# A gated-attention kernel: the row-tiled products of a group in one run, with another set of order keys

## The chip, the cores and the metric

The kernel runs on one core of a Trainium2 chip. The metric is the device time of one execution in microseconds (us). Five engines take part, each working through its own list of instructions in order: TensorE (PE, matrix products), VectorE (DVE), ScalarE (ACT), GpSimd (POOL) and SyncE (SP), which here issues nearly all DMA transfers. Engines wait for each other only through semaphores.

## The reference, cut to what matters

```python
xn = layernorm(x)                                  # x: 4 batch rows x 512 positions x 256
Q = xn @ Wq + bq                                   # 16 heads of 128
K, V = xn @ Wk + bk, xn @ Wv + bv                  # 4 key heads; each serves 4 query heads
attn = softmax(Q @ K.T / sqrt(128) + causal_mask)  # per head, 512 x 512
ctx = attn @ V
y = gelu(ctx @ Wo + bo)
s = layernorm(xn + y) * gamma + beta
g = silu((silu(gate) * up) @ w_down.T)             # gate, up = halves of xn @ w_gate_up.T
out = x + s * g
```

Everything is float32. The kernel writes each float32 operand of most products as a sum of a leading part and a rest in a shorter format, and forms three products per pair (leading x leading, leading x rest, rest x leading).

## The kernel before, in words

Up to about 101 us the kernel loads and splits weights, normalizes x and runs the feed-forward part of the earlier batch rows. Attention then runs in 16 groups, one for each batch row (4) and key head (4): `ph = b * 4 + g`, in `order.run()`. A group has these steps; the short names are those of the tasks.

- `Qp`, `Kp`, and once a batch row `Vp`: projections on TensorE, copied out of PSUM in two parts by ACT (`Qh`, `Kh`, `Vh`) and DVE (`Ql`, `Kl`, `Vl`). The four `Qp` of a group use the four PSUM banks `bank0` to `bank3`.
- `Sp` (line 703): scores. A product covers 32 queries of each of the four heads against the keys that they may see; 4 row blocks `i` of 128 queries with 4 such products `t` each, into PSUM tiles `ps`, of which there are two. `M` on DVE adds the mask and takes the row's least value, `E` on ACT takes the exponential into the tile `p` and sums the row, `R` on DVE inverts the sum, and `N` (line 746) on POOL normalizes.
- `T` (line 760) on DVE transposes a 128 x 512 piece of `p` in 32 x 32 blocks into one of four tiles `u`. `H` (line 789) on ACT copies its leading part to `pT`, and `L` (line 792) on POOL writes the rest. There are ten such pieces in a group, (i, j) with key tile j not above row block i: four for j = 0, three for j = 1, two for j = 2, one for j = 3.
- `W` (`weighted`, line 798): the weights times the values, as products with 32 rows in four row tiles of the array at once, one for each head, adding up in `bank0` to `bank3`. The values of a group, `vr`, are loaded in two halves by SP (`values_beside`, line 663; four transfers for each half).
- `Ch` on ACT and `Cl` on DVE copy the banks to `ctxT`; `Y` on TensorE multiplies with `w_o`, adding up over the four groups of a batch row in `py`.
- After a batch row's last group, `O`, `G` and the `F` tasks (partly on POOL) form GELU, the second normalization and the output.

The order of all instructions is fixed when the program is written. The class `Order` holds a list of tasks, each with its engine, an estimated duration, a key, the tasks that it comes after, and places in rings that it takes and gives back. `Order.run` (line 81) plays them through: whenever an engine is free, it emits the ready task with the smallest key. `keep` chains each engine's instructions in the order found. The estimates set only this order; on the chip an instruction waits for the data and buffers that it really uses. The keys are sums of the numbers in `KEYS` and of the group number; for instance, where `ph` is the group:

```python
key = ph - 0.3 + K["t0"] + K["t1"] * j + K["t2"] * i       # T
... key + K["h"] ...  key + K["l"]                          # H, L
ph + (K["w0"] if ph + 2 < NPH else K["lw"]) + K["w1"] * m   # W
base = ph - 0.5 + K["s0"] + ... K["s1"] * i                 # Sp, M, E
```

How many runs `W` is cut into is set by `RUNS` (line 24): each entry is a list of key tiles whose products are emitted without anything between. Four places use it:

```python
runs = ((3,), (2,), (1,), (0,)) if last else RUNS            # line 1119
deps = [(x, b, g, i, j) for j in run for i in range(j, NT) for x in "HL"] + [("vr", b, g, j // 2) for j in run]
done_w[ph] = {j: ("W", b, g, m) for m, run in enumerate(runs) for j in run}   # line 1135
slot = [done_w[ph - 1][j]] if ph else ...                    # line 1114: what H of tile j waits for
```

So a run comes after the `H` and `L` of its own tiles, and the next group's `H` for tile j comes, in the planned order, after the run that holds j. `Ch` comes after a group's last run. The loads of `vr` come after the runs of the group before that hold the same tiles. The last group (15) always has four runs, one tile each. The tiles `pT` and `vr` and the loaded weights `w_q` and `w_o` share 13 buffers of one kind.

Of the kernel before, what the change touches and what calls it, by code (L numbers as in the profile page):

```python
# [19 lines left out]
EPS = 1e-5  # L20
S = 32
MASK = -1e9
KEYS = {"q0": 1.294, "q1": -0.162, "k": 1.154, "v0": 2.242, "v1": -0.947, "s0": -2.531, "s1": 0.181, "s2": -0.026, "n": -5.223, "t0": -5.822, "t1": 3.68, "t2": 2.849, "h": 1.078, "l": -1.275, "w0": -1.75, "w1": -0.111, "c": 3.151, "y0": 0.375, "y1": 1.022, "f0": 1.31, "f1": 4.659, "wo": 28.733, "wq": 2.307, "vr": 3.547, "ls": 2.337, "lt": -16.381, "lc": 7.543, "lw": 2.356, "da": 2.973, "db": 1.284}
RUNS = ((0, 1), (2, 3))
ON_ACT = (0, 1)
HIGHEST = 3.4028235e38

# [132 lines left out]
def kernel(  # L160
# [803 lines left out]
    for name, n in (("s", 2), ("u", 4), ("ctx", 3), ("gate", 2), ("stage", 1)):  # L964
        order.ring(name, n)
    K = KEYS
    weights, done_w = {}, {}
# [52 lines left out]
    for ph in range(NPH):  # L1020
# [97 lines left out]
        last = ph + 1 == NPH  # L1118
        runs = ((3,), (2,), (1,), (0,)) if last else RUNS
        for m, run in enumerate(runs):  # L1120
# [125 lines left out]
```

## Time and profile before

| what | value |
|---|---|
| median of 3 runs | 639.38 us (638.06 to 639.59) |
| the profiled execution, its own time | 637.73 us |
| its span, first to last instruction | 635.8 us |
| mean granted TensorE clock | 0.994 |
| TensorE matmul, busy | 616.7 us (97%) |
| POOL, DVE, ACT, busy | 455.7, 417.6, 405.0 us |
| row-tiled products (`bank<-pT,vr`) | 3072, 120.7 us busy |
| score products (`ps<-kT,qT`) | 576, 115.0 us busy |
| output products (`py<-w_o,ctxT`) | 768, 112.7 us busy |

A line of the profile names an engine, an operation and its tiles as out<-in. Nearly all lines stand under L49, because the helper at line 49 records every instruction; the tile names tell them apart. Matmuls are pipelined and overlap, so the length of a step on TensorE is read from one step's start to the next step's start, not from busy time. PEclk is the granted TensorE clock, 1.00 being full speed. "x192" counts instructions. In a table by stretch each engine's busy us are followed by its number of instructions.

### The profile page before, as it was taken

What the parts mean: (1) busy time and instruction counts of PE and PEld (TensorE: products, weight loads), DVE (VectorE), ACT (ScalarE), POOL (GpSimd) and SP (SyncE); (2) the same over time, 40 slices, a digit from 0 to 9 for tenths busy, and PEclk for the clock granted to TensorE, in tenths of its full rate; (3) what the DMA queues carried; (4) which work ended last, traced back from release to release, by engine and by line L of the source; (5) the groups of instructions that cost most, each with busy time, mean ns of one, the idle gap of its engine ahead of it and who ended that gap; (6) DMA issues with size and microseconds to landing.
All of it is one profiled execution on the core that took longest, in us unless ns stands there. A gap on an engine that the chain in (4) does not pass through costs nothing.

```text
span 635.8 us, 15865 instructions
## 1 busy us (share of the span) xinstructions
PE 616.7 (97%) x6004; PEld 552.4 (87%) x6004; DVE 417.6 (66%) x1131; ACT 405.0 (64%) x1025; POOL 455.7 (72%) x595
## 2 busy tenths in 40 slices
PE   7999998999999999999999999999999999999994
PEld 6888886988988889899888989888999988998894
DVE  5974517465439585668669584877767587768635
ACT  3542415484259686778858595977668598758652
POOL 4698778173516985949599794959996586999653
PEclk9999998999999999999999999999999999999998
DMA  6867788407398369553967867196947818774900
GB/s 206 275 197 242 269 283 283 159 4 204 103 318 220 111 163 257 165 138 95 294 186 174 241 175 234 34 299 182 231 170 184 245 55 253 174 197 109 262 5 34
DMA packets 86236, 118.09 MB, mean 186 GB/s; under 512 B 5648, under 2 KB 72336, under 8 KB 82064
## 3 DMA queue, kind: packets, MB, share of 16 engines
q1 hardware_dynamic: 86160, 117.08, 64.0%
q8 instruction: 47, 0.77, 0.5%
q14 instruction: 29, 0.24, 0.1%
HBM read 87.70 MB, written 29.36 MB: 184 GB/s over the span
## 4 chain that ended last, share of the span: by engine, by line
PE 65%; POOL 12%; DMA 9%; DVE 6%; issue 4%; ACT 2%; SPq 2%; POOLq 0%; DVEq 0%; ACTq 0%
PE bank L49 30%; PE ps L49 13%; PE py L49 10%; POOL pT L49 4%; PE pd L49 4%; PE pv L49 3%; PE pk L49 3%; DMA vr<-v_dram 3%; POOL p L49 2%; DMA fin_dram<-gate 1%; DMA xT_dram<-xT 1%; DVE p L49 1%; DMA fin<-fin_dram 1%; POOL gate L539 1%; POOL w_d L246 1%
## 5 line engine op out<-in xcount | busy, mean ns | idle before, releaser
L49 POOL TENSOR_SCALAR p<-p,total 128x384 f32<-128x384 f32 (+7 forms) x248 | 118.7, 499 | 68.9 <-DVE total L49 68.6
L49 ACT ACTIVATE p<-p,least 128x192 f32<-128x192 f32 (+15 forms) x256 | 131.7, 516 | 56.8 <-DVE least L49 52.0
L49 DVE CUSTOM_DVE_ANT_0 p<-ps,mask 128x192 f32<-128x192 f32 (+15 forms) x256 | 104.4, 431 | 77.7 <-PE ps L49 76.5
L49 PE MATMUL bank<-pT,vr 32*128 32x128 f32 (+15 forms) x3072 | 120.7, 307 | 0.2 <-DMA vr<-v_dram 0.2
L49 PEld LDWEIGHTS bank<-pT,vr 32*128 32x128 f32 x3072 | 113.0, 184 | 7.6 <-issue 2.9
L49 PE MATMUL ps<-kT,qT 128*128 128x512 f32 (+11 forms) x576 | 115.0, 332 | 3.0 <-DVE least L49 2.4
L49 POOL TENSOR_TENSOR pT<-u,pT 128x512 fp32r<-128x512 f32 x83 | 107.2, 1299 | 12.1 <-ACT pT L49 10.7
L49 PE MATMUL py<-w_o,ctxT 128*128 128x256 f32 x768 | 112.7, 286 | 1.1 <-DVE ctxT L49 1.0
L49 POOL TENSOR_TENSOR pT<-u_more,pT 128x512 fp32r<-128x512 f32 x77 | 99.6, 1299 | 13.3 <-PE bank L49 8.3
L49 PEld LDWEIGHTS py<-w_o,ctxT 128*128 128x128 f32 x768 | 103.2, 189 | 4.3 <-DVE ctxT L49 1.5
L49 PEld LDWEIGHTS ps<-kT,qT 128*128 128x128 f32 x576 | 87.0, 188 | 14.1 <-DVE least L49 8.0
L49 PE MATMUL bank<-xT_again,w_q 128*128 128x512 f32 x384 | 95.0, 393 | 0.0
L49 PEld LDWEIGHTS bank<-xT_again,w_q 128*128 128x128 f32 x384 | 71.3, 189 | 14.2
L49 ACT CAST pT<-u 128x512 fp32r<-128x512 f32 x83 | 51.3, 619 | 26.4 <-DVE u L49 20.4
L49 DVE STREAM_TRANSPOSE u<-p 128x512 f32<-128x512 f32 x83 | 57.7, 698 | 10.2 <-POOL p L49 9.0
L49 DVE STREAM_TRANSPOSE u_more<-p 128x512 f32<-128x512 f32 x77 | 54.0, 701 | 13.7 <-POOL p L49 8.0
L49 ACT ACTIVATE ctxT<-bank,bv_sb 128x512 fp32r<-128x512 f32 x64 | 42.3, 683 | 27.1 <-PE bank L49 25.2
L49 ACT CAST pT<-u_more 128x512 fp32r<-128x512 f32 x77 | 47.1, 619 | 13.6 <-DVE u_more L49 8.5
L49 DVE SCALAR_TENSOR_TENSOR ctxT<-bank,bv_sb,ctxT 128x512 fp32r<-128x512 f32 x64 | 46.3, 738 | 9.5 <-ACT ctxT L49 9.5
L49 POOL TENSOR_TENSOR y<-y,fin 128x256 f32<-128x256 f32 x40 | 29.5, 739 | 29.7 <-ACT y L49 11.8
L49 DVE SCALAR_TENSOR_TENSOR qT<-bank,bq_sb,qT 128x384 fp32r<-128x384 f32 x64 | 38.5, 602 | 18.3 <-ACT q L49 18.2
L49 ACT ACTIVATION_READ_ACCUMULATOR p<-p,least 128x1 f32 x256 | 48.2, 188 | 0.0
(134 smaller groups left out, 951.0 us busy)
## 6 DMA issues: line engine op xcount, KB each, us to landing
vr<-v_dram SPq DMA_DIRECT2D x128, 256.0 KB, 7.0
w_q<-w_dram_q SPq DMA_DIRECT2D x15, 1024.0 KB, 5.3
w_o<-w_dram_o SPq DMA_DIRECT2D x15, 1024.0 KB, 10.0
v_dram<-v SPq DMA_DIRECT2D x16, 512.0 KB, 3.6
fin<-fin_dram SPq DMA_DIRECT2D x16, 384.0 KB, 5.5
xT_dram<-xT SPq DMA_DIRECT2D x8, 512.0 KB, 4.9
fin_dram<-gate SPq DMA_DIRECT2D x16, 256.0 KB, 4.3
xT_again<-xT_dram SPq DMA_DIRECT2D x8, 512.0 KB, 4.2
```

The source lines that it names most:

```text
L49: made = getattr(self.engine, name)(*args, **kw)
L246: lo_on.tensor_tensor(dst[1], src, dst[0].bitcast(F32), ALU.subtract)
L539: pool.tensor_tensor(g[:, 1 + k], g[:, 0], gb_sb[:, k], ALU.mult)
```

## The change

`RUNS` has one entry in place of two: the row-tiled products of all four key tiles form one run, which comes after all ten `H` and `L` and after both halves of `vr`. `done_w` then names this one run for every tile. All thirty numbers in `KEYS` are other ones; among them `w0` goes from -1.75 to -6.162, `h` from 1.078 to 7.725, `s0` from -2.531 to -1.292 and `q0` from 1.294 to 0.186. The last group's four runs stay. No instruction is added or taken out.

```diff
--- before.py
+++ after.py
@@ -20,8 +20,8 @@
 EPS = 1e-5
 S = 32
 MASK = -1e9
-KEYS = {"q0": 1.294, "q1": -0.162, "k": 1.154, "v0": 2.242, "v1": -0.947, "s0": -2.531, "s1": 0.181, "s2": -0.026, "n": -5.223, "t0": -5.822, "t1": 3.68, "t2": 2.849, "h": 1.078, "l": -1.275, "w0": -1.75, "w1": -0.111, "c": 3.151, "y0": 0.375, "y1": 1.022, "f0": 1.31, "f1": 4.659, "wo": 28.733, "wq": 2.307, "vr": 3.547, "ls": 2.337, "lt": -16.381, "lc": 7.543, "lw": 2.356, "da": 2.973, "db": 1.284}
-RUNS = ((0, 1), (2, 3))
+KEYS = {"q0": 0.186, "q1": 0.188, "k": 1.276, "v0": 2.664, "v1": -0.427, "s0": -1.292, "s1": 0.081, "s2": 0.03, "n": -5.947, "t0": -4.154, "t1": 2.359, "t2": 2.218, "h": 7.725, "l": -1.068, "w0": -6.162, "w1": 1.004, "c": 3.429, "y0": 0.388, "y1": 1.235, "f0": 1.568, "f1": 3.265, "wo": 26.284, "wq": 4.081, "vr": 4.774, "ls": 2.625, "lt": -17.512, "lc": 4.554, "lw": 2.179, "da": 4.28, "db": 1.598}
+RUNS = ((0, 1, 2, 3),)
 ON_ACT = (0, 1)
 HIGHEST = 3.4028235e38
```

## The prediction

> **What bounds the kernel now.** I read the page's busy shares first, then a table of busy times by stretch, then TensorE's timeline around the row-tiled products.
>
> ```profile
> span 635.8 us, 15865 instructions
> PE 616.7 (97%) x6004; PEld 552.4 (87%) x6004; DVE 417.6 (66%) x1131; ACT 405.0 (64%) x1025; POOL 455.7 (72%) x595
> ```
>
> A busy share alone proves little, so here are four groups of the second batch row, one group to a line (from the start of one group's first run of row-tiled products to the next). The columns are the stretch, its length, and the busy us of each engine.
>
> ```profile
> core 0: us, PE busy (x) PEld busy (x) DVE busy (x) ACT busy (x) POOL busy (x), PEclk, DMA share, GB/s
> 327.45:356.40 28.95, 28.77 (x352) 26.27 (x355) 20.56 (x67) 20.58 (x62) 27.60 (x38) 1.00 0.72 197
> 356.40:385.30 28.90, 28.90 (x329) 26.09 (x325) 19.65 (x51) 20.52 (x52) 23.12 (x29) 1.00 0.75 218
> 385.30:414.30 29.00, 29.00 (x305) 26.90 (x298) 20.66 (x69) 22.21 (x65) 19.56 (x27) 1.00 0.39 107
> 414.30:443.25 28.95, 28.66 (x317) 25.19 (x316) 21.95 (x60) 22.90 (x51) 21.83 (x31) 1.00 0.88 245
> ```
>
> TensorE idles 0.5 us of 115.8 here. So between about 105 and 595 us the time is the length of TensorE's instruction stream; only what shortens or stalls that stream counts. POOL stands second and in the first of these lines (groups 5, 9 and 13, where the previous batch row's final normalization is also done) it is at 27.60 of 28.95.
>
> Now the price of one change between 128-row and 32-row products. TensorE's timeline (start, length, what, how many):
>
> ```profile
> 354.21 4.64 PE L49 MATMUL bank<-pT,vr 32*128 32x512 f32 x96
> 358.79 0.95 PE L49 MATMUL ps<-kT,qT 128*128 128x256 f32 x6
> 359.67 2.88 PE L49 MATMUL bank<-pT,vr 32*128 32x256 f32 x96
> 362.47 0.79 PE L49 MATMUL ps<-kT,qT 128*128 128x192 f32 x5
> ```
> ```profile
> 304.18 7.27 PE L49 MATMUL bank<-pT,vr 32*128 32x512 f32 x192
> 311.38 0.83 PE L49 MATMUL ps<-kT,qT 128*128 128x416 f32 x3
> ...
> 412.58 0.84 PE L49 MATMUL ps<-kT,qT 128*128 128x256 f32 x6
> 413.26 0.53 PE L49 MATMUL py<-w_o,ctxT 128*128 128x256 f32 x3
> ```
>
> From start to next start, the split group takes 4.58 (tiles 0 and 1) + 0.88 (two score products between) + 2.80 (tiles 2 and 3) = 8.26 us. In one stretch the 192 products take 311.38 - 304.18 = 7.20, and the same two score products, among 128-row neighbours, 413.26 - 412.58 = 0.68: together 7.88. One round trip into row tiles and back costs 8.26 - 7.88 = **0.38 us**.
>
> **The change, part by part.**
>
> *Two runs become one.* The timeline shows which groups are really split. Groups 1, 4, 8 and 12 already run as one stretch (starts 215.75, 304.18, 420.20, 536.04), because their second run happened to be placed straight after the first. Group 15 keeps its four runs in both kernels. Eleven groups are split (0, 2, 3, 5, 6, 7, 9, 10, 11, 13, 14). Removed: 11 x 0.38 = **4.2 us** of TensorE's stream. No product, load or copy is removed or added; 3072 row-tiled products stay.
>
> *The new wait.* The run now needs all ten probability tiles, so TensorE's row-tiled products of key tiles 0 and 1 wait for the last tile's split on POOL (1.30 us each). Behind that wait on TensorE's queue stand the next group's scores, and this group's context copies on ACT and DVE, its output products and the queries two groups on. What must fill TensorE until then? In group 6 the first run started at 354.21 and the second at 359.67, so at most 4.6 us of other work must be drawn forward. The next group's score rows 1 and 2 are at hand: they stand right behind the first run today (331.96 to 336.7 in group 5, 4.7 us), and DVE and ACT have 6 to 9 us of slack per group. I take 0. If that cover is gone, the cost is up to 4.6 us a group.
>
> *Splits come later.* In the planned order, a next group's splits for tiles 0 and 1 may start only after the whole run, not after its first part. Between two runs there would be 28.95 - 0.38 - 7.20 = 21.4 us. Ten splits take 13.0 us, normalizing row 3 takes 2.5 (four at 0.63), and the first copy on ACT 0.6: 16.1 us, hidden with 5 us to spare. In groups 5, 9 and 13 the cover is thin (second rival).
>
> *The keys.* `w0` from -1.75 to -6.16 puts the run ahead of the next group's scores (key ph-2.03 before, ph-0.79 after, against ph-1.75 and ph-6.16 for the run): the scores no longer slip in between. `h` from 1.08 to 7.73 puts the first copies of turned tiles behind the next group's exponentials on ACT. Late next: the split on POOL, then the run. Bounded by one or two exponentials (0.6 us each) per tile below, by ACT's idle 6 to 8 us a group above; ACT's slack absorbs it, so I take 0, the nearer end, with up to +1 us a group where POOL is full. `q0`, `k`, `v0`, `y1` reorder fillers among themselves; the same products are issued, so 0, with single stalls of the 0.2 us kind seen at 335.60 either way.
>
> *The sync queue.* Both halves of the values beside the weights (`vr`, eight transfers) now follow the end of the whole run. Their issue took 5.4 us at 423.56 and 10.6 at 185.37, landing 7.0: 12 to 18 us, against the 21 us until the next run. Hidden; if not, a stall like those before the runs of groups 8 and 12 follows, where today the first stretch takes 7.87 and 7.73 instead of 7.20 (0.67 and 0.53 us). `vr` at 4.77 instead of 3.55 stands later against output loads; `wq` and `wo` move it among 1 MB loads. Bounds: -1.2 us (both stalls vanish) to +2; I take 0.
>
> *Start and end.* Up to 101.6 us the order isn't planned by keys, and group 0's splits were done by 178, before its run at 182.34: 0. At the end, group 14's run ended at 594.67, yet the first split of group 15 began only at 598.56, behind row 3, whose last scores stood between the runs. With one run these may come before it (gain up to 3.9) or behind it (loss up to 2.8, the length of the second run). I take 0 and keep both ends.
>
> **Sum.** Against the profiled execution's own 637.73 us (span 635.8 and 1.9 around it): 637.7 - 4.2 = 633.5. The median shown is 639.38, 1.65 above it: 635.2. For new short stalls I allow 0.3, about two of the 0.2 us kind: **635.5 us**, 0.6% under the median. From no change this measurement can tell about 0.3%, or 1.9 us.
>
> **A rule against the change.** TensorE idles little now, and one run per group invites a wait of microseconds. Today's nearest row is the stretch 96.0 to 101.6, with 2.50 us of idle before 101.59:
>
> ```profile
> 96.00:101.60 5.60, 3.10 (x15) 2.04 (x13) 3.90 (x6) 2.53 (x7) 5.42 (x8) 1.00 0.75 237
> 102.80:106.20 3.40, 3.40 (x11) 2.74 (x11) 2.76 (x4) 1.86 (x4) 1.83 (x2) 0.50 0.91 299
> ```
>
> The granted clock then fell to 0.50 for 3.4 us, which costs 1.7 us. The Trainium skill ("TensorE: Matmul & The Clock Gate", section "Why this matters for your kernels") says to avoid idle gaps above about 3 us. Here 2.5 us with thin work before it was enough, so the measurement decides: a stall of 2.5 us or more is priced at itself plus 1.7; gaps up to 1.0 us (at 193.29) left the clock at 1.00. With stalls of 0.2 us the rule adds nothing and the sum stands at 635.5; were three groups to wait 3.7 us each (below), it would add 5.1.
>
> **Rivals.**
>
> *POOL becomes the bound, slower.* Place: the runs of groups 5, 9 and 13. While TensorE is in one stretch, POOL finds little to do:
>
> ```profile
> 304.18:311.38 7.20, 7.20 (x193) 7.04 (x192) 3.10 (x12) 6.22 (x13) 1.93 (x3) 1.00 1.03 364
> 420.88:428.07 7.19, 7.19 (x190) 7.03 (x190) 3.00 (x11) 5.54 (x12) 2.80 (x5) 1.00 1.02 351
> 536.59:543.76 7.17, 7.17 (x189) 7.02 (x189) 3.09 (x11) 5.67 (x13) 2.76 (x5) 1.00 1.04 360
> 215.75:222.96 7.21, 7.21 (x194) 7.03 (x193) 1.92 (x4) 3.07 (x9) 6.41 (x9) 1.00 0.41 114
> ```
>
> If it does only 2.5 us (mean of the first three) under a run, 27.6 - 2.5 = 25.1 remain for the 21.4 between runs: 3.7 us late in each of three groups, 11.2 in all. 639.4 - 4.2 + 11.2 = 646.4, and 651.5 if each wait also halves the clock. It decides once the three waits sum to 4.2, 1.4 each, that is when POOL does less than 27.6 + 7.2 - 28.6 - 1.4 = 4.8 us under the run. For it: POOL waited 68.6 us for row sums in all, so it starves just when scores pause. Against: in group 1's stretch it did 6.41 us, since splits start as soon as a tile's products are through, and the normalization's steps are not urgent: groups 6 and 7 leave POOL 5.8 and 9.4 us free.
>
> *The gain is given back in small waits, no measurable change.* 0.2 to 0.4 us at each run, as TensorE's stream is drawn forward against score masks (0.18 at 335.60): 11 x 0.3 = 3.3, giving 638.5.
>
> *The end gains too.* Row 3 of group 15 ahead of group 14's run: 3 us more, 632.5.
>
> **How the numbers follow.** The forecast (633.5 to 637.4) 0.41; the end gaining too 0.05; given back 0.15; slower 0.39, mostly spread from 641.3 to 647, as partial stalls are likelier than all three in full. Faster 0.46, same 0.15, slower 0.39. Leaving out about 0.05 below and 0.12 above gives 632.5 to 646.5.
>
> **What would show it.** Right: row-tiled products in stretches of 192 for every group but the last, each some 7.2 us; a group's period near 28.6; TensorE's idle from 105 to 595 us still under 3 us. Wrong: idle before row-tiled products released by `pT` from POOL above 1 us in groups 5, 9, 13; granted clock at 0.50 inside the groups; or score products waiting for `least`. The forecast fails if the waits sum to more than 4.2 us, and is too timid if the end also moves.

## The result: slower by 4%, and the profile after

The changed kernel takes **664.5 us** (663.9 to 665.9, 4 runs) against 638.7 us of the kernel before on the same chip, a ratio of 1.041 with a 95% interval of 1.039 to 1.044. The forecast was 635.5; the range ended at 646.5. Even the rival that named a slower time (646.4 to 651.5) was too low.

The page of the changed kernel, its first two lines:

```profile
span 664.0 us, 15854 instructions
PE 631.5 (95%) x6004; PEld 557.1 (84%) x6004; DVE 422.2 (64%) x1131; ACT 408.1 (61%) x1025; POOL 454.4 (68%) x595
```

The same instructions take the same time on DVE, ACT and POOL (all within 5 us of before). TensorE is "busy" for 14.8 us more although its 6004 products are the same, and idles for 13.4 us more besides. Here are the four groups of the second batch row, from each run's start to the next (columns as before: stretch, length, busy us of each engine, then granted clock, DMA share and GB/s):

```profile
312.97:342.69 29.72, 26.57 (x307) 23.24 (x306) 20.91 (x60) 19.67 (x53) 27.09 (x38) 1.00 0.71 223
342.69:371.59 28.90, 28.50 (x315) 25.01 (x315) 21.54 (x66) 20.55 (x58) 25.66 (x35) 1.00 0.67 193
371.59:397.98 26.39, 26.39 (x309) 24.10 (x308) 16.83 (x46) 18.92 (x47) 18.79 (x23) 1.00 0.65 161
397.98:434.83 36.85, 36.45 (x354) 31.49 (x353) 25.44 (x74) 27.86 (x72) 20.65 (x28) 1.00 0.55 154
```

These lines can be compared with those of the prediction only in sum (see the first point on the prediction). The batch row takes 121.86 us instead of 116.02 (start of group 4's run to start of group 8's), and TensorE idles 3.9 us of it instead of 0.5. Along the kernel the loss is: 1.6 us before the first run, 7.2 in groups 0 to 3, 5.8 and 6.0 in the next two batch rows, 7.6 from group 12's run to the end; together 28.2, the difference of the spans of the two profiled executions (the medians differ by 25.8).

Overlapping matmuls hide short waits in busy time, so I summed for each kind of product the time from its start to the next product's start, over the second batch row:

| us per batch row | before | after |
|---|---|---|
| row-tiled products | 29.35 | 28.78 |
| scores | 28.96 | 32.36 |
| output products | 24.55 | 27.32 |
| queries | 22.06 | 22.01 |
| keys and values | 11.10 | 11.39 |

The runs themselves did what was forecast. They are shorter by 0.57 in sum, and the products next to a run, each some 0.1 longer than its neighbours of the same shape, cost 0.8 instead of 1.4. The scores lost 3.4 and the output products 2.8. A wait is counted here with the product before it, so some 1.2 of these 2.8 are waits of the scores that follow (0.98 and 0.23 below). Group 5 shows how, on TensorE's timeline; a bracket gives the idle time just before and what ended it:

```profile
323.65 1.45 PE L49 MATMUL py<-w_o,ctxT 128*128 128x256 f32 x10 [1.59 <-DVE ctxT L49]
...
334.82 0.63 PE L49 MATMUL ps<-k,q 128*128 128x32 f32 x4 [0.98 <-ACT q L49]
335.26 0.60 PE L49 MATMUL py<-w_o,ctxT 128*128 128x256 f32 x3
336.10 0.46 PE L49 MATMUL ps<-k,q 128*128 128x96 f32 x2 [0.23 <-DVE least L49]
...
338.11 3.59 PE L49 MATMUL ps<-kT,qT 128*128 128x224 f32 x18
341.97 0.79 PE L49 MATMUL ps<-kT,qT 128*128 128x384 f32 x3 [0.27 <-DVE least L49]
342.69 7.27 PE L49 MATMUL bank<-pT,vr 32*128 32x512 f32 x192
```

After the run of group 4 TensorE waits for the context copies; then output products and queries are used up; then the next group's scores stand almost in one block from 334.82 to 342.69, right ahead of the run. Before, group 5's first run stood just after row block 0 of the scores:

```profile
326.82 0.63 PE L49 MATMUL ps<-k,q 128*128 128x64 f32 x4
327.38 4.65 PE L49 MATMUL bank<-pT,vr 32*128 32x512 f32 x96
331.96 0.95 PE L49 MATMUL ps<-kT,qT 128*128 128x256 f32 x6
```

Two views of waits tell the same. The mask `M` on DVE writes `least` as it empties a score tile, so scores that wait for `least` wait for a free tile. TensorE's weight loads for scores, waiting for DVE, in the kernel before and in the changed one (total us, times, longest):

```profile
PEld ps L49 <- DVE least L49: 8.9, 24, 0.8
```
```profile
PEld ps L49 <- DVE least L49: 22.5, 61, 1.2
```

And ACT and POOL, again before and then in the changed kernel:

```profile
ACT ctxT L49 <- PE bank L49: 25.2, 16, 5.5
POOL pT L49 <- ACT pT L49: 15.8, 8, 8.2
```
```profile
ACT ctxT L49 <- PE bank L49: 84.9, 16, 6.4
...
POOL pT L49 <- ACT pT L49: 51.1, 19, 8.2
```

ACT stands at a context copy until the run ends, with the next group's first copies `H` queued behind it, and POOL waits for those.

### The profile page after: what moved, and what is told of

The parts are those of the page before. It is cut to its first block, busy times and chain, and to the rows that moved or that the text cites. A ratio compares the mean times of both kernels' runs of the same rounds, so it can differ in the third digit from the quotient of the medians.

```text
span 664.0 us, 15854 instructions
## 1 busy us (share of the span) xinstructions
PE 631.5 (95%) x6004; PEld 557.1 (84%) x6004; DVE 422.2 (64%) x1131; ACT 408.1 (61%) x1025; POOL 454.4 (68%) x595
## 4 chain that ended last, share of the span: by engine, by line
PE 58%; POOL 11%; DMA 11%; DVE 8%; ACT 4%; issue 3%; SPq 2%; POOLq 0%; DVEq 0%; ACTq 0%
PE bank L49 26%; PE ps L49 12%; PE py L49 10%; POOL p L49 3%; PE pd L49 3%; PE pv L49 3%; DMA fin_dram<-gate 3%; DVE p L49 2%; ACT p L49 2%; DMA fin<-fin_dram 2%; PE pk L49 2%; DMA st_q<-in_wq_dram 1%; POOL pT L49 1%; DMA xT_dram<-xT 1%; POOL y L49 1%
## 5 line engine op out<-in xcount | busy, mean ns | idle before, releaser
L49 ACT ACTIVATE p<-p,least 128x128 f32<-128x128 f32 (+15 forms) x256 | 132.2, 518 | 31.9 <-DVE least L49 29.3
L49 POOL TENSOR_SCALAR p<-p,total 128x288 f32<-128x288 f32 (+3 forms) x248 | 118.4, 497 | 34.7 <-DVE total L49 34.2
L49 DVE CUSTOM_DVE_ANT_0 p<-ps,mask 128x128 f32<-128x128 f32 (+15 forms) x256 | 107.8, 434 | 52.7 <-PE ps L49 49.1
L49 POOL TENSOR_TENSOR pT<-u_more,pT 128x512 fp32r<-128x512 f32 x81 | 104.2, 1295 | 48.6 <-ACT pT L49 33.7
L49 PE MATMUL ps<-kT,qT 128*128 128x256 f32 (+11 forms) x576 | 125.5, 348 | 7.4 <-DVE least L49 6.3
L49 POOL TENSOR_TENSOR pT<-u,pT 128x512 fp32r<-128x512 f32 x79 | 101.4, 1293 | 30.6 <-ACT pT L49 17.4
L49 PE MATMUL bank<-pT,vr 32*128 32x128 f32 (+15 forms) x3072 | 117.7, 306 | 2.6 <-issue 2.6
L49 PEld LDWEIGHTS ps<-kT,qT 128*128 128x128 f32 x576 | 91.1, 196 | 25.6 <-DVE least L49 20.6
L49 ACT ACTIVATE ctxT<-bank,bv_sb 128x512 fp32r<-128x512 f32 x64 | 41.1, 687 | 91.1 <-PE bank L49 84.9
L49 PEld LDWEIGHTS bank<-xT_again,w_q 128*128 128x128 f32 x384 | 70.3, 188 | 13.4
L49 DVE STREAM_TRANSPOSE u_more<-p 128x512 f32<-128x512 f32 x81 | 56.8, 702 | 25.5 <-POOL p L49 11.7
L49 ACT CAST pT<-u_more 128x512 fp32r<-128x512 f32 x81 | 50.1, 625 | 16.7 <-DVE u_more L49 15.9
```

The costliest lines, as they stand in the source:

```text
L49: made = getattr(self.engine, name)(*args, **kw)
```

## The experiments

My theory after the result was that one long run is itself the cause: TensorE loses the first run as work for a time in which nothing else is ready. The rival was the other keys. Times are medians; the kernel before, run beside each set, had 638.5 to 639.1.

**One run with the old keys, two runs with the new ones.**

```diff
-RUNS = ((0, 1), (2, 3))        # keys of before kept
+RUNS = ((0, 1, 2, 3),)
```

> One run of all four key tiles, with the keys of the kernel before. If the one run itself is the cause (TensorE loses the first run, 4.6 us, as work for the time in which the next queries are copied and the next scores can't start; scores then stand in one block ahead of the run and wait for their two PSUM tiles), the time is 655 to 675 us. If the other keys are the cause, it is near my forecast, 634 to 637 us.

Measured: 670.2 us (662.2 to 673.4), ratio 1.043 (1.033 to 1.053), that is some 27 us lost (21 to 34).

The reverse keeps `RUNS = ((0, 1), (2, 3))` and takes all thirty keys of the changed kernel.

> Two runs as before, with the changed kernel's keys. If the one run is the cause, most of the loss goes: 638 to 648 us, the rest being keys that were set for another order. If the keys are the cause, the time stays at 655 us or more.

Measured: 713.6 us, ratio 1.118 (1.112 to 1.124). So the one run alone, with the keys of before, costs about what the whole change costs. Given one run, the other keys make no difference that can be told (1.043 against 1.041). With two runs the new keys are ruinous, which I had not expected: `w0` at -6.16 places the runs so early that TensorE stops inside them. Waits of that kernel between 300 and 460 us:

```profile
PEld bank L49 <- POOL pT L49: 6.3, 2, 5.6
```

Its mean granted clock was 0.939 as well. But this kernel is no clean reverse: in its trace the two runs stand in one stretch in eleven of the fifteen groups. It shows what these keys do, not what two separate runs would cost under them. That the cut alone is enough for the loss rests on the first of the two kernels.

**Wait for all, but let the next group go on early.** Keys of before and two tasks, of which the first needs all ten pieces and the second follows at once.

```diff
+need = run if last or m else range(NT)
-deps = [(x, b, g, i, j) for j in run for i ... ] + [("vr", b, g, j // 2) for j in run]
+deps = [(x, b, g, i, j) for j in need for i ... ] + [("vr", b, g, j // 2) for j in need]
-    ph + ... + K["w1"] * m
+    ph + ... + K["w1"] * m - 100.0 * (m > 0 and not last)
```

> Keys of before; the products of all four tiles start only when all ten pieces are split, and the second part follows the first at once, but in the planned order the next group's first copies may follow the first part already. If the loss comes from the wait for all ten pieces (TensorE's work runs out before), this is as slow as one run with the same keys, within 3 us. If it comes from the next group's splits being let go 2.8 us later, it is within 5 us of the kernel before.

Measured: 672.5 us, ratio 1.053 (1.048 to 1.058), no faster than one run. To let the next group's copies go earlier in the planned order won nothing back.

**The move alone.** These kernels keep the order of before, with every other engine's list unchanged, and hold back the first run until the second is emitted, so that the two stand together on TensorE.

```diff
-lambda: [weighted(b, g, j, ...) for j in run]
+lambda: held_back(n == 2 and m == 0, [lambda j=j: weighted(b, g, j, ...) for j in run])
+def held_back(hold, emits):
+    held.extend(emits)
+    while held and not hold:
+        held.pop(0)()
```

> The order of the kernel before on every engine, except that on TensorE the first run of a group is moved back to stand right before the second: nothing else is reordered, eleven changes of tiling are saved. My forecast's step (the score products drawn forward cover the wait, cost 0) gives 638.7 - 4.2 = 634.5 us. If the delay of the first run by 0.9 to 4.7 us holds up the copies that need its buffers and its successors, it is slower than before: 640 to 655 us.

Measured: 660.7 us, ratio 1.034 (1.029 to 1.040): eleven changes of tiling saved, 22 us lost. The forecast assumed that this move costs nothing, and it does not hold. Group 5 in this kernel, first TensorE, then POOL:

```profile
327.86 0.53 PE L49 MATMUL py<-w_o,ctxT 128*128 128x256 f32 x3
330.79 1.50 PE L49 MATMUL ps<-kT,qT 128*128 128x192 f32 x6 [2.40 <-DVE least L49]
332.09 0.92 PE L49 MATMUL py<-w_o,ctxT 128*128 128x256 f32 x3
332.81 2.53 PE L49 MATMUL ps<-kT,qT 128*128 128x384 f32 x9
336.17 0.67 PE L49 MATMUL ps<-kT,qT 128*128 128x288 f32 x3 [0.83 <-DVE least L49]
336.76 6.08 PE L49 MATMUL bank<-pT,vr 32*128 32x512 f32 x148
```
```profile
330.85 1.28 POOL L49 TENSOR_TENSOR pT<-u,pT 128x512 fp32r<-128x512 f32 x1
339.73 1.29 POOL L49 TENSOR_TENSOR pT<-u_more,pT 128x512 fp32r<-128x512 f32 x1 [7.60 <-PE bank L49]
```

TensorE stops for 2.40 us where the first run used to stand, and POOL's splits stop for 7.60 us until the moved run has read its tiles and their buffers `pT` come free. In the kernel before POOL went on without a break:

```profile
331.38 1.29 POOL L49 TENSOR_TENSOR pT<-u,pT 128x512 fp32r<-128x512 f32 x1
332.63 1.29 POOL L49 TENSOR_TENSOR pT<-u_more,pT 128x512 fp32r<-128x512 f32 x1
```

**Where it is moved far, and where little.** The same hold in some groups only:

```diff
-n == 2 and m == 0
+n == 2 and m == 0 and b * KV + g in (5, 9, 13)      # or in (2, 6, 10)
```

> All of the computation; the first run moved back only in groups 5, 9 and 13, where it moves by 4.7 us (against 0.9 us in groups 2, 6 and 10, which made no difference). If the loss grows with how long the run is held back, most of the 22 us of moving all eleven is here: 652 to 660 us. If it is spread evenly over the moved groups, a quarter: 643 to 646 us.

> The first run moved back only in groups 2, 6 and 10, where 0.88 us of scores stood between the runs and the full move showed no new stall at the run itself: 3 x 0.38 = 1.1 us less than before by the price of a round trip, 637 to 638 us, hardly to be told from no change. If even a delay of 0.9 us holds up the splits, it is slower by 1 us or more.

Measured: 656.4 us for groups 5, 9 and 13, ratio 1.029 (1.024 to 1.034), that is 18 of the 22 us in three of the eleven groups; and 638.5 us for groups 2, 6 and 10, ratio 1.000 (0.999 to 1.002), no change to be told. This fits a loss that follows the length of the delay, 4.7 us against 0.9. But groups 5, 9 and 13 are also those where POOL has most to do, and the two were not tried apart. The 1.1 us that the three saved round trips promised did not show in the time, though each run's stretch on TensorE had its 7.2 us.

TensorE stopped for 2.40 us in each of the three groups, and each stop came with a fall of the granted clock (last of the columns but two):

```profile
333.00:339.80 6.80, 5.12 (x19) 4.49 (x19) 3.21 (x14) 3.10 (x12) 2.64 (x3) 0.50 0.24 65
455.90:466.10 10.20, 8.85 (x49) 7.46 (x53) 3.09 (x14) 3.72 (x13) 2.31 (x2) 0.50 0.14 41
582.20:585.50 3.30, 3.30 (x14) 2.99 (x12) 1.78 (x10) 2.09 (x9) 3.30 (x4) 0.50 1.09 241
```

TensorE was busy for 17.3 us in them, so they are worth up to 8.6 of the 21.3 us that this execution, the slowest of four, took more than the median before. The three stops are another 7.2.

**Free buffers.** Two causes are mixed in the moved kernel: late buffers and a missing filler. More buffers don't fit in memory, so I freed some by leaving work out: the first group's query weights serve as both weights from the second group on, one half of the first group's values serves as all values, and their loads are left out (thirty weight loads, not 28 as I wrote, and 124 value transfers). The sizes and order of all products stay.

```diff
-to[ph] = work.tile([P, 2, 1024], F32R, tag="w", bufs=13, ...)
-sp.dma_start(to[ph].bitcast(F32), w_dram[kind, g])
+to[ph] = wqs[0]
+if (b, g, h) != (0, 0, 0):
+    vr[b, g, h] = vr[0, 0, 0]
+    return
```

> The control: the order of the kernel before with the same loads left out and the same buffers free. TensorE was busy without a gap, so little should change: 634 to 639 us by both theories (the stalls of 0.7 and 0.5 us for late values go).

> As the kernel with the first run moved back, but two or more of the 13 shared buffers are left free: every later group uses the first group's query weights for both weights and one half of the first group's values for all values, and their loads are left out (28 weight loads and 124 value transfers; the output is that of other weights and values). If the late return of the weights' buffers pT is what holds up the splits and through them TensorE, this is no slower than the same kernel with the order of before and free buffers, and up to 4.2 us faster. If TensorE simply lacks the first run as filler while the scores wait for their PSUM tiles, it stays 12 us or more slower than that one.

> The changed kernel with the same loads left out and buffers free. If the buffers alone cause the loss there too, 632 to 640 us. If its order itself (all scores of the next group in one block ahead of the run, the splits behind the context copies on ACT) holds TensorE up, it stays at 650 us or more.

Measured: the order of before 635.8 us (ratio to the kernel before 0.995, 0.993 to 0.997); with the first run moved back 648.6 (1.017, 1.014 to 1.019); the changed kernel 650.5 (1.019, 1.016 to 1.021). Against their control the moved order still loses 12.8 us, the changed one 14.6, where with scarce buffers it was 22 and 25.8. So free buffers and missing loads together are worth about 9 and 11 us, and most of the loss is something else; my expectation "buffers alone" fell. In the changed kernel the output products are back at 24.15 us a batch row, the scores stay at 32.26.

Where do the 11 us lie in the changed kernel? Mostly between the runs of groups 4 and 5, 8 and 9, 12 and 13. Here is the first of these stretches, from the end of one run to the start of the next, in the changed kernel and with free buffers:

```profile
320.16:342.69 22.53, 19.38 (x118) 16.24 (x114) 17.09 (x48) 17.04 (x46) 22.45 (x30) 1.00 0.63 197
```
```profile
321.07:340.32 19.25, 18.90 (x118) 16.16 (x114) 15.21 (x43) 16.86 (x46) 19.17 (x24) 1.00 0.17 55
```

POOL, the last of the five columns, works nearly without a break in both (22.45 of 22.53 us, 19.17 of 19.25), and TensorE idles 3.15 us in the first. Under the run ahead of it POOL had done only 4.64 us of work, against 6.66 with free buffers. It had stood waiting for `fin`, an input of the previous batch row's final normalization, until 313.96:

```profile
313.96 1.60 POOL L49 TENSOR_TENSOR y<-y,fin 128x256 f32<-128x256 f32 x2 [7.55 <-DMA fin<-fin_dram]
```

SP issued these loads 5.1 us before the run of group 4, behind four transfers of `vr`; where `vr` is left out, it issued them 10.6 us before that run. The two other stretches go from 22.45 and 23.19 us to 19.26 and 19.25. Together that is 10.4 of the 14.4 us between the spans of these two kernels. So in the traces the changed kernel gains mostly time on POOL, and not room for `pT`. Free buffers and missing loads weren't tried apart.

What is left in the moved order is plain in group 5. DVE, then TensorE, with free buffers:

```profile
329.00 0.71 DVE L49 STREAM_TRANSPOSE u_more<-p 128x512 f32<-128x512 f32 x1 [1.38 <-POOL p L49]
329.63 0.39 DVE L49 CUSTOM_DVE_ANT_0 p<-ps,mask 128x256 f32<-128x256 f32 x1
```
```profile
327.18 0.52 PE L49 MATMUL py<-w_q,ctxT 128*128 128x256 f32 x3
330.09 0.90 PE L49 MATMUL ps<-kT,qT 128*128 128x192 f32 x6 [2.39 <-DVE least L49]
```

The mask of row block 1's scores stands in DVE's list behind the transposition of row block 0, which needs that block's whole chain: mask, exponential, sum, normalization on POOL. Until then neither score tile comes back. The 4.6 us of row-tiled products used to stand over just this chain.

**The block of scores in the changed kernel.** Two ways to give score tiles back sooner, each with its control and with free buffers: DVE masks only half of the keys, or there is a third PSUM tile for scores (its bank freed by mixing the output sums).

```diff
+n = seen // 2 if i and (b, g) != (0, 0) else seen     # mask and copy :n instead of :seen
```
```diff
+third = (b, g) >= (0, 2) and (i * NT + t) % 3 == 2
-ps = psum.tile([P, L], F32, tag="s", bufs=2, ...)
+ps = psum.tile([P, L], F32, tag="y1" if third else "s", bufs=1 if third else 2, ...)
```

> The changed kernel with free buffers (650.5 us), and from the second group on DVE masks and copies only the first half of each row's keys for row blocks 1 to 3, so that a score tile is given back sooner (left out: the other half's scores; the output is wrong by that too). If the block of scores ahead of the run is paced by DVE's emptying of the two PSUM tiles, 636 to 645 us; if not, 648 us or more.

> The control: the order of before with free buffers (635.8 us) and the same halved masking. Where scores are spread between other products their tiles don't pace TensorE, so it gains 3 us at most: 632 to 637 us. If halved masking speeds any order up alike, it gains as much as the changed order does.

> The changed kernel with free buffers (650.5 us) and a third PSUM tile for scores from group 2 on, the order of every engine's instructions unchanged. (To free a PSUM bank, all four output row blocks of a batch row add up in two regions of one bank, so the output sums are mixed.) If the rest of the loss is TensorE waiting for one of two score tiles to come back, 636 to 643 us. If it is waiting for something else in that block (the next queries' copies, the row chain on the other engines), it stays at 647 us or more.

> The control: the order of before with free buffers (635.8 us) and the same third score tile. Its scores stand between other products, so little is to be had: 632 to 636 us.

Measured:

| with free buffers | order of before | changed order | difference | scores, us per batch row |
|---|---|---|---|---|
| nothing more | 635.8 | 650.5 | 14.6 | 28.93 and 32.26 |
| half masks | 630.3 | 640.4 | 10.1 | 27.75 and 29.96 |
| third score tile | 632.3 | 646.0 | 13.7 | 28.05 and 30.63 |

Halved masking takes 10.1 us off the changed order, as expected, but 5.5 off its control, where I had expected 3 at most. So halved masks take 4.5 us off the 14.6. A third tile explains about 1, within the scatter: the number of tiles isn't what paces the block. Half masks shorten the chain mask, exponential, sum and so on too, a third tile doesn't; that fits a bound by DVE's own work in the block, but isn't shown apart.

## Why the prediction was wrong, point by point

*What bounds the kernel* was right: before the change TensorE's stream sets the time, and the loss is found as waits and slow stretches in it. But the four lines of that table are equal slices of about 28.95 us and not, as I wrote, stretches from one first run to the next; the first runs of groups 5 to 8 started at 327.38, 354.21, 382.62 and 420.20. The sum is right; the share of POOL in each group is not to be read from them. Of my signs of being wrong, the clock at 0.50 and scores waiting for `least` came; row-tiled products waiting for `pT` from POOL did not.

*Two runs become one, 4.2 us saved.* The size was right where it can be read: 192 products in 7.20 us in group 6, and 0.57 + 0.6 = 1.2 us less a batch row for three split groups, 0.4 each. It is far smaller than what the move cost.

*The new wait, "I take 0".* This step failed. I asked whether enough work was at hand and counted the next group's scores of row blocks 1 and 2. They are at hand as instructions, but their masks stand behind row block 0's chain, and I didn't ask how fast they could run one after another. Where I put 0, the moved kernel showed stops of 2.40 us, with TensorE waiting for a score tile. Moving the first run back in three groups alone cost 18 us, 6 each, above even the upper end of 4.6 that I gave: the granted clock fell as well, for 20.3 us in the profiled execution.

*Splits come later, "hidden with 5 us to spare".* Failed too. I counted ten splits and one row's normalization, 15.5 us of work on POOL, and left out the other rows' normalization and the end of the previous batch row. In the changed kernel POOL worked 22.45, 19.26, 16.68 and 18.92 us between the five runs from group 4's to group 8's, and the first of these filled its stretch. I also took the buffers as given: in group 5 of the moved kernel POOL stood still for 7.60 us until the run had read its tiles.

*The keys, 0.* Given one run, the times tell nothing against it, but the intervals leave room for some 7 us either way. With the run they put `H` behind the context copies on ACT (84.9 us of waiting there, 47.7 with one run and the keys of before) and the scores almost into one block; this order is 14.6 us worse than that of before even with buffers free.

*The sync queue, 0.* The loads of `vr` did not hold up the runs of groups 5, 9 and 13. But I priced only whether `vr` itself comes late. Its transfers stand ahead of `fin`, and POOL waits for `fin` just where it has most to do: 7.55 us in the changed kernel (5.84 at the same place before). With `vr` and the weights not loaded, 10.4 us went there.

*The clock rule.* I priced it only for waits of 2.5 us or more, having seen 1.0 us pass unharmed. In group 1 of the changed kernel waits of 0.50 and 0.99 us were followed by the half clock:

```profile
212.15 0.93 PE L49 MATMUL ps<-kT,qT 128*128 128x192 f32 x6 [0.50 <-DVE least L49]
214.07 1.24 PE L49 MATMUL ps<-kT,qT 128*128 128x288 f32 x6 [0.99 <-DVE least L49]
```
```profile
214.70:221.50 6.80, 5.85 (x28) 4.68 (x30) 3.70 (x14) 4.03 (x13) 5.76 (x9) 0.50 0.09 35
```

Such stretches (214.7 to 221.5, 579.9 to 583.3, 624.3 to 631.1) sum to 17.0 us between the first planned group and the end of the last. TensorE was busy for 15.9 of them, so they are worth up to 8 us of the 28.2; before there were none there. The one at 624 follows a stall of 2.61 us inside group 14's run, for which the trace names nothing. With it that is up to 6 of the 7.6 us lost from group 12's run on; it is gone with free buffers, and why it stood there is not settled. That the wait of 1.00 us at 193.29 did no harm was luck, as the last section shows.

*The rival.* Its sign was right, and in good part its mechanism: ahead of groups 5, 9 and 13 POOL did 4.64, 4.73 and 5.44 us of work under the run, where less than 4.8 was to decide it, and then nearly filled the stretch to the next run. But no run waited there for POOL's last split. In the chain of waits POOL holds up the turned tiles, these the copies of the next queries on ACT, and these the scores ahead of the run. Groups 5, 9 and 13 are only part of the loss, and a faster POOL was not tried.

*The end.* From the end of group 14's run the changed kernel took 40.1 us against 41.1 before, though the granted clock was 0.50 for 6.8 us of it. With free buffers it was 38.0, and 41.0 in the order of before: a gain of 3 us, as the third rival had it. The 7.6 us lost from group 12's run on lie before that.

What stays open: with buffers free and half masks, 10 us between the two orders. By the run starts about 4 lie before group 0's run, 4 in groups 0 to 3 and 5 in the two batch rows after, with 2 regained at the end. Which wait each of these is was not tried apart. No version tested beats the kernel before with all its work done.

## What to carry to other kernels

Where an engine is the bound and never idle, its instructions are each other's cover: before moving a block, ask what chain on other engines it stands over, and not only whether other instructions are at hand. Then count all that the second engine has to do between two blocks, not only the chain that you think of, and ask what it can do under the block. A long block also holds its inputs' buffers to its end, so price the move by when they come back. Here a saving of 0.4 us per group was bought with waits of microseconds.

## What the runs showed of the hardware

The length of a wait alone did not decide whether the granted clock fell. Near 193 us eight of these kernels have the same wait of TensorE, 0.97 to 1.00 us before an output product. In the kernel before and in the two with all first runs moved back the clock stayed at 1.00; in five others (the order of before with free buffers, with half masks and with the third tile, and the two with some groups moved) it went to 0.50 for 3.4 or 6.8 us. First the kernel before, then the order of before with free buffers:

```profile
193.29 0.38 PE L49 MATMUL py<-w_o,ctxT 128*128 128x256 f32 x1 [1.00 <-DVE ctxT L49]
193.30:196.70 3.40, 3.40 (x25) 3.25 (x26) 3.19 (x12) 2.57 (x10) 1.44 (x4) 1.00 1.11 227
```
```profile
194.19 0.39 PE L49 MATMUL py<-w_o,ctxT 128*128 128x256 f32 x1 [0.99 <-DVE ctxT L49]
194.60:198.00 3.40, 3.40 (x16) 3.40 (x17) 2.63 (x9) 2.46 (x9) 1.44 (x2) 0.50 0.01 2
```

Of the nine stops of 2.4 us in the three kernels with the run moved back by 4.7 us, eight came with a stretch at 0.50, and one did not (at 449.44 with free buffers). Waits of 1.59 us at 323.65 and 1.49 us at 445.45 in the changed kernel left the clock at 1.00. So in these kernels a wait's effect on the clock could be priced only as a chance.

A round trip from 128-row to 32-row products and back cost 0.38 to 0.4 us; the product next to the change took some 0.2 us where its neighbours took 0.1.
